# Two edits to the order of a mixture-of-experts and local-attention kernel: where the next token norms stand beside a softmax, and which queue loads the experts' second biases

## The chip, the cores and the metric

The kernel runs on one core of a Trainium2 chip. The core has a matrix engine (TensorE, "PE"), a vector engine (VectorE, "DVE"), a scalar engine (ScalarE, "ACT"), a general engine (GpSimd, "POOL") and a sync engine (SyncE, "SP"), each with an instruction queue of its own that it works through in order. SP, ACT and POOL can start DMA transfers; a transfer that has to wait for something holds everything behind it in the queue that issues it. The metric is the device time of one execution in microseconds (us).

## The reference

The input `x` is 16 x 256 tokens of 512 features, with a context tensor of the same shape and an index `itok` of a key position for each token. All is float32. Four residual layers follow each other, each behind a layer norm:

```
x = x + conv_attention(norm(x), k, skip, ctx)          # a long convolution over the features
x = x + experts(norm(x))                               # 8 experts, top 2, and a shared expert
x = x + local_attention(norm(x), ctx, itok)            # 16 heads, keys itok-8 .. itok
x = x + ffn(norm(x))                                   # 512 -> 2048 -> 512, gelu
```

The two layers that the change touches, cut to what matters:

```
# experts: the top 2 of 8 logits, softmax over the two
h = gelu(x @ w1[e] + b1[e])
routed = sum over the 2 experts of gate * (h @ w2[e] + b2[e])

# local attention
q_c = x @ W_dq;   kv_c = kv @ W_kvc
scores = (q_nope . k_nope + rope(q_rope) . rope(k_rope)) * scale
scores = where(itok - 8 <= key <= itok, scores, -1e30)
out = softmax(scores) @ v;   out @ W_o
```

## The kernel before, in words

The class `Kernel` writes one program. A scheduler puts the instructions of each engine in an order derived from the order in which they are written, and sets the waits between engines. The engine queues then run in that compiled order. `tc.issue_after(instruction)` around a piece of code makes what is written in it be placed behind the named instruction.

**Stages.** `conv_shared` does the first layer, the routing and the shared expert. `routed` runs the experts. `attention_sorted` does the local attention on tokens sorted by key position, and `ffn` the last layer. Data goes between the stages through DRAM: `x1d` holds the tokens after the first layer and the shared expert, `xgd` the normed rows grouped by expert, `ygd` the experts' results, `x3s` the tokens after attention.

**Around the bias load.** At its end `conv_shared` sends the last token rows to `xgd` by scattering (L437 on POOL's queue), writes zeros behind each expert's last row (eight scatters, also L437), and stores the tokens to `x1d` (L574, on SP's queue). `routed` then loads `e_b2`, the second biases of all experts for all 128 partitions, 2 MB, from a DRAM row that the kernel made before (L658 on VectorE is the last of the work that it waits for). Behind it come, on SP's queue, the expert tiles `xg`: `load` (L958) takes 128 rows of `xgd`, four tiles are in flight, and each load waits for the scatters of rows and zeros that could write them. PE transposes an expert tile (L972, `ptg`), multiplies it with `w1` (L983, `phg`), transposes the result (L994), ACT applies gelu (L996), and PE multiplies with `w2` (L1002, `pog`). The bias `b2` is added at the end (L1011) on VectorE, and the row stored to `ygd` (L1014). Between the expert tiles, `beside` prepares the attention's weights (loads `pre`, L1120).

**The attention.** There are 32 tiles T of 128 tokens, taken in groups of four. For one group: `tokens` makes the tile's input. It adds the two routed results, each times its gate, to the row of `x1d` (two L1542 on VectorE; the rows of `ygd` come by gathers on POOL's queue, L2005), takes the layer norm (L66, L68 and L72 on VectorE, L70 and L71 on POOL), transposes the rotary rows on PE (L1550, `prr`, copied at L1551) and the normed tile (L99, `pt`, copied by ACT at L100). `latents` makes the query latents (L1561, L1572), and `heads` makes the queries of two pairs of heads (L1589 to L1600 on PE; L1605 and L1613 copies on ACT; L1607 on VectorE; L1608 and L1609 on POOL).

For each tile, the loop in `attention_sorted` writes, in this order: `scores` (L1651, L1657 on PE), `weigh` (the first half of the softmax on VectorE: L1667 transpose, L1669 mask, L1673 maximum, L1674 subtraction), `tokens` of tiles of the next group, `values` of the tile before (L1697 `pu` on PE, copied at L1703), `weights` (the exponential, L1678 on ACT; the sum L1680, reciprocal L1682, product L1683 and transpose L1685 on VectorE), `window` of the tile after (key transposes, L1623 `pkw` and L1628 `prw` on PE; mask pieces L1636 to L1639 on VectorE), in the first two tiles the head pairs of the second half of group 0, and `project` of the tile two before (L1713 `po` on PE, 32 matmuls).

In the first group (g = 0) `tokens` of the next group's tiles is called for its tiles 0 and 1 at t = 1 and t = 2, and for its tiles 2 and 3 at t = 3. The scheduler is free to place the instructions of these calls on VectorE ahead of the softmax beside which they are written, as soon as their data is expected. In later groups the calls stand at another place (the end of the loop's body) and are not touched.

Of the kernel before, what the change touches and what calls it, by code (L numbers as in the profile page):

```python
# [13 lines left out]
ALU = mybir.AluOpType  # L14
# [4 lines left out]
P = 128  # L19
# [15 lines left out]
CQ, WIN = 8, 32  # L35
# [7 lines left out]
class Kernel:  # L43
# [888 lines left out]
    def routed(self, xgd, ygd, early):  # L932
        nc, tc, a = self.nc, self.tc, self.a
        with ExitStack() as ctx:
# [10 lines left out]
            ps_o = pool("e_ps_o", 2, space=PSUM)  # L945
            w1, w2 = self.e_w1, self.e_w2
            b2 = bp.tile([P, E, D], F32, name="e_b2")
            nc.sync.dma_start(b2, self.b2d.partition_broadcast(P))
            more = lambda i, half: self.beside(i, half, heads, early)

            def load(i):
# [24 lines left out]
            def hidden(i, xT):  # L976
                e = nc.values_load(
                    self.expert[0:1, i : i + 1], engines=[mybir.EngineType.PE], min_val=0, max_val=E - 1,
                    skip_runtime_bounds_check_because="a sum of a one-hot row over 0 to E - 1",
                )  # L980
                ph = ps_h.tile([P, EH], F32, tag="h", name="phg")
                for c in range(DC):
                    nc.tensor.matmul(  # L983
                        ph, xT[:, c, :], w1[:, c, bass.ds(e * EH, EH)], start=(c == 0), stop=(c == DC - 1)
                    )
                hs = tp.tile([P, EH], F32, tag="hs", name="hs")
                nc.vector.tensor_copy(hs, ph)
                return e, hs
# [30 lines left out]
            for i in range(NT):  # L1019
                if i + 2 < NT:  # L1020
                    xg[i + 2] = load(i + 2)
                e, hs = hidden(i, xT.pop(i))
# [452 lines left out]
    def attention_sorted(self, fetched, ygd, x3s, end_of_queries):  # L1475
        nc, tc = self.nc, self.tc
# [7 lines left out]
        with ExitStack() as ctx:  # L1484
# [50 lines left out]
            def tokens(st, t):  # L1535

                T = st["g"] * T4 + t
                if t == 0:
                    st["xT"], st["rope"] = g_xT, g_rope
                xt, yts, rr = xs[T], st["y"][t], rrs.pop(T)  # L1540
                for k in range(2):
                    nc.vector.scalar_tensor_tensor(  # L1542
                        xt, yts[k], self.routes[:, T, 2 + k : 3 + k], xt, ALU.mult, ALU.add
                    )
                xh = tp.tile([P, D], F32, tag="xh", name="xh")
                self.layernorm(xh, xt, small)
                toks = slice(t * P, (t + 1) * P)
                pt = ps_m.tile([P, 2, P], F32, tag="m", name="prr")
                for i in range(2):
                    nc.tensor.transpose(pt[:, i, :], rr[:, i, :], self.ident)  # L1550
                nc.scalar.copy(st["rope"][:, :, toks], pt)  # L1551
                self.transposed(st["xT"][:, :, toks], xh, ps_m, "m")
# [60 lines left out]
                        nc.scalar.copy(qn[:, cs, c0 : c0 + CQ], by_chunk(pqn[k][i]))  # L1613
                return turned

            wins, last_at = {}, [None]

            def window(T):
                gw = gws.pop(T)
# [21 lines left out]
            def scores(st, T):  # L1641

                w, t = wins[T], T % T4
                s = ps_s.tile([P, 4 * P], F32, tag="s", name="ps")
                for a in range(4):
                    for piece in range(3):
                        for j in range(4):
                            c = t * 16 + a * 4 + j
                            r = slice(j * WIN, (j + 1) * WIN)
                            if piece == 0:  # L1650
                                nc.tensor.matmul(  # L1651
                                    s[r, a * P : (a + 1) * P], w["kn"][:, a, r], qn[:, c, :],
                                    start=(a == 0), stop=False, skip_group_check=True,
                                )
                            else:
                                c0 = a * P + (piece - 1) * (P // 2)
                                nc.tensor.matmul(  # L1657
                                    s[r, c0 : c0 + P // 2], krz[piece - 1][:, a, r], qr[:, c, :],
                                    start=False, stop=True, skip_group_check=True,
                                )  # L1660
                return s

            def weigh(T, s):

                e = ap_.tile([P, 16, WIN], F32, tag="e", name="e")
                flat = e.rearrange("p x k -> p (x k)")
                nc.vector.transpose(flat, s)  # L1667
                e4 = e.rearrange("p (a h) k -> p a h k", h=4)
                nc.vector.tensor_tensor(  # L1669
                    e4, e4, wins[T]["mask"].unsqueeze(2).to_broadcast([P, 4, 4, WIN]), ALU.add  # L1670
                )
                mx = small.tile([P, 16], F32, tag="mx", name="mx")
                nc.vector.tensor_reduce(mx, e, AX.X, ALU.max)  # L1673
                nc.vector.tensor_tensor(e, e, mx.unsqueeze(2).to_broadcast([P, 16, WIN]), ALU.subtract)  # L1674
                return e

            def weights(e):
# [70 lines left out]
            for T in range(NT_ + 2):  # L1748
                g, t = T // T4, T % T4
                if T < NT_:  # L1750
                    if 3 <= T + 2 < NT_:
                        fetch_keys(T + 2)
                    s = scores(state[g], T)
                    e = weigh(T, s)
                    nxt = state.setdefault(g + 1, new(g + 1)) if g + 1 < NG else None

                    if nxt is not None:
                        for k in () if g == 0 else ((0,), (2,), (), ())[t]:
                            fetch((g + 1) * T4 + k)
                            fetch_routed(nxt, k)  # L1760
                    if nxt is not None and g == 0 and 1 <= t <= TH:
                        tokens(nxt, t - 1)
                    if nxt is not None and g == 0 and t == 3:
                        for k in range(TH, T4):
                            tokens(nxt, k)
                    if nxt is not None and t == 3:
                        latents(nxt)
                if 1 <= T <= NT_:
                    uts[T - 1] = values(T - 1, ats.pop(T - 1))
                if T < NT_:  # L1770
                    ats[T] = weights(e)
                    if T + 1 < NT_:
                        window(T + 1)
                    if T < 2:
                        for two in range(T * HP // 4, (T + 1) * HP // 4):
                            turned = heads(state[0], two, parts[1])
                    if nxt is not None and g == 0 and 1 <= t <= TH:
                        with tc.issue_after(turned):
                            fetch(T4 + TH + t - 1)
                            fetch_routed(nxt, TH + t - 1)  # L1780
                    if nxt is not None and t == 3:
                        for two in range(HP // 2):
                            heads(nxt, two)
                if T >= 2:
                    project(state[(T - 2) // T4], T - 2, uts.pop(T - 2))
                if T >= NT_:

                    if T == NT_:
                        end_of_queries()
                    which = T - NT_  # L1790
                    xT = self.e_w2[:, which * DC * N : (which + 1) * DC * N].rearrange("p (c x) -> p c x", c=DC)
                    for k in range(T4):
                        xt = ap_.tile([P, N], F32, tag="sw", name="xt", bufs=3)
                        nc.sync.dma_start(xt, x3s[which][k * P : (k + 1) * P, :])
                        xh = tp.tile([P, D], F32, tag="xh", name="xh")
                        self.layernorm(xh, xt, small)
                        self.transposed(xT[:, :, k * P : (k + 1) * P], xh, ps_m, "m")
                if T < NT_ and nxt is not None:
                    if g > 0:
                        if t == 0:  # L1800
                            fetch((g + 1) * T4 + 1)
                            fetch_routed(nxt, 1)
                        for k in ((0,), (1,), (2, 3), ())[t]:
                            tokens(nxt, k)
                        if t == 1:
                            fetch((g + 1) * T4 + 3)
                            fetch_routed(nxt, 3)
# [365 lines left out]
```

## Time and profile before

| | |
|---|---|
| median of 3 runs | 3021.12 us (3020.19 to 3021.73) |
| profiled execution | 3020.16 us, span 3018.4 us |
| PE busy | 2947.3 us (98%) |
| VectorE busy | 1461.7 us (48%) |
| POOL busy | 1112.7 us (37%) |
| ACT busy | 694.4 us (23%) |
| granted TensorE clock, mean | 0.995 |
| DMA | 209.87 MB, mean 70 GB/s |

The span is the time from the first to the last instruction of the profiled execution; its own time of 3020.16 us is 1.76 us longer. Rows of a list in order of time read: start, busy time, engine, line, operation, what it writes and reads, how many instructions were merged into the row, and in square brackets the idle time of the engine ahead of it with what ended it. All of these are in us from the start of the span. Rows of the granted clock give a share of full speed.

The bias load was issued at 902.58 and landed 9.1 us later. The attention's first tiles T = 0 to T = 3 stand at about 1278, 1298, 1315 and 1336 us.

### The profile page before, as it was taken

Reading aid. Unit: us, or ns where it says so; the run is one execution under the profiler, and the core shown is the slowest. Engines: PE = TensorE matmul, PEld = TensorE weight load, DVE = VectorE, ACT = ScalarE, POOL = GpSimd, SP = SyncE. Lnnn points to the kernel's source line nnn. Section 1 sums busy time; section 2 is a strip of 40 time slices with the busy share of each in tenths; the row PEclk is TensorE's granted clock in tenths of the full one; section 3 lists DMA queues with packets and bytes.
Section 4 is the critical chain, followed back from the end, with each engine's and each line's share of the span. In section 5 each row is a group of like instructions: output and inputs, shape, how many; then the busy total and the mean of one; then the engine's idle time right before and its main releaser. Section 6 shows DMA issues by size and latency. Waiting matters only on the chain.

```text
span 3018.4 us, 34924 instructions
## 1 busy us (share of the span) xinstructions
PE 2947.3 (98%) x12697; PEld 1499.5 (50%) x12697; DVE 1461.7 (48%) x2652; ACT 694.4 (23%) x1314; POOL 1112.7 (37%) x1462
## 2 busy tenths in 40 slices
PE   8999999999999999889999999999999999999998
PEld 4444444445446666544454455455444444444443
DVE  7978778778764444343343343343432223222222
ACT  2222112212211111333433333333211111111110
POOL 4566556455450300465555555543120300301101
PEclk9999999999999999999999999999999999999999
DMA  4231221221136733221131131112210100100100
GB/s 124 74 116 61 71 75 49 66 79 54 43 114 188 224 129 128 92 75 45 51 92 44 48 92 49 46 57 84 103 54 14 56 14 14 56 11 18 39 0 29
DMA packets 119219, 209.87 MB, mean 70 GB/s; under 512 B 27592, under 2 KB 47976, under 8 KB 118400
## 3 DMA queue, kind: packets, MB, share of 16 engines
q1 hardware_dynamic: 90752, 125.63, 13.9%
q0 software_dynamic: 28288, 81.92, 8.4%
q8 instruction: 104, 1.70, 0.2%
q14 instruction: 75, 0.61, 0.1%
HBM read 140.12 MB, written 67.37 MB: 69 GB/s over the span
## 4 chain that ended last, share of the span: by engine, by line
PE 80%; DVE 8%; issue 5%; POOL 4%; DMA 2%; ACT 0%; POOLq 0%; SPq 0%; DVEq 0%; ACTq 0%
PE po L1965 15%; PE ph L1907 13%; PE po L1713 11%; PE y L327 6%; PE phg L983 4%; PE pog L1002 4%; PE pqn L1592 4%; PE m L327 3%; PE pout L569 3%; PE ph L556 2%; PE pqr L1589 2%; DVE oT L332 2%; PE pqn L1600 2%; PE pt L99 2%; DVE kv L283 1%
## 5 line engine op out<-in xcount | busy, mean ns | idle before, releaser
L1713 PE MATMUL po<-nw,w 128*128 128x512 f32 x1024 | 445.7, 593 | 0.0
L1965 PE MATMUL po<-p,ht 128*128 128x512 f32 x1024 | 445.1, 592 | 0.0
L327 PE MATMUL y<-kv,ut 128*128 128x512 f32 x768 | 352.9, 595 | 9.3 <-DVE pr L338 9.3
L1713 PEld LDWEIGHTS po<-nw,w 128*128 128x128 f32 x1024 | 192.1, 190 | 235.1 <-issue 229.6
L1965 PEld LDWEIGHTS po<-p,ht 128*128 128x128 f32 x1024 | 192.7, 190 | 233.4 <-issue 232.0
L1907 PE MATMUL ph<-w,w 128*128 128x512 f32 x640 | 281.2, 592 | 0.0
L1969 DVE TENSOR_TENSOR res<-res,po 128x512 f32<-128x512 f32 x128 | 87.7, 685 | 315.4 <-PE po L1965 315.4
L327 PEld LDWEIGHTS y<-kv,ut 128*128 128x128 f32 x768 | 143.1, 191 | 183.3 <-issue 163.6
L1907 PEld LDWEIGHTS ph<-w,w 128*128 128x128 f32 x640 | 121.5, 190 | 152.6 <-issue 152.6
L283 DVE TENSOR_TENSOR kv<-pvt,cT 128x512 f32<-128x512 f32 x256 | 170.3, 682 | 0.5 <-PE pvt L267 0.5
L2005 POOL DMA_INDIRECT w<-ygd,slot_s x64 | 72.3, 1130 | 257.8 <-DMA pre<-in_W_uvT_dram 204.3
L2005 POOL DMA_INDIRECT gw<-kvd,keys_of x128 | 133.7, 1045 | 51.9 <-issue 37.3
L1607 DVE TENSOR_TENSOR w<-pqr,w 128x512 f32<-128x512 f32 (+1 forms) x72 | 45.3, 631 | 203.8 <-ACT sw L1605 188.1
L332 DVE TENSOR_REDUCE oT<-pr 128x64 f32<-128x512 f32 x192 | 131.8, 686 | 6.6
L983 PE MATMUL phg<-w,xTg 128*128 x568 | 134.6, 380 | 0.2
L1002 PE MATMUL pog<-w,hT 128*128 x284 | 133.6, 593 | 0.0
L70 POOL TENSOR_TENSOR ln_rs<-ln_mv,eps 128x1 f32<-128x1 f32 x64 | 13.0, 202 | 320.5 <-DVE ln_mv L68 316.0
L556 PE MATMUL ph<-xT,w_s 128*128 128x512 f32 x256 | 118.5, 607 | 0.0
L1921 ACT ACTIVATE ht<-ht,p1b 128x512 f32<-128x512 f32 x96 | 69.3, 722 | 212.8 <-DVE ht L1926 212.8
L293 POOL TENSOR_TENSOR w<-kv 128x512 f32<-128x512 f32 x64 | 81.2, 1269 | 100.0 <-DVE kv L283 70.8
L1592 PE MATMUL pqn<-w,m 128*128 128x512 f32 (+1 forms) x288 | 117.7, 552 | 0.3 <-DVE w L1569 0.3
L1907 PE MATMUL ph<-xT,w 128*128 128x512 f32 x256 | 116.4, 592 | 0.0
(305 smaller groups left out, 4509.1 us busy)
## 6 DMA issues: line engine op xcount, KB each, us to landing
xg<-xgd SPq DMA_DIRECT2D x71, 256.0 KB, 2.7
ygd<-y SPq DMA_DIRECT2D x71, 256.0 KB, 2.0
xt<-in_x_dram SPq DMA_DIRECT2D x32, 256.0 KB, 3.4
ct<-in_ctx_dram SPq DMA_DIRECT2D x32, 256.0 KB, 3.3
ut<-in_kt_dram SPq DMA_DIRECT2D x32, 256.0 KB, 2.7
w<-in_w_dram SPq DMA_DIRECT2D x8, 1024.0 KB, 5.8
x1d<-xt SPq DMA_DIRECT2D x32, 256.0 KB, 3.0
x3s<-xt POOLq DMA_DIRECT2D x32, 256.0 KB, 2.7
```

The source lines that it names most:

```text
L283: nc.vector.tensor_tensor(c["kv"][half][:, mc, :].rearrange("p (b j i) -> p b j i", i=NH, j=NH), c["vt"][:, mc, cols].rearrange("p (b i) - ...
L327: c["conv"] = nc.tensor.matmul(y, t, v, start=(start and k == 0), stop=(k == len(terms) - 1), skip_group_check=True).ins
L332: nc.vector.tensor_reduce(c["oT"][:, lc, cols].rearrange("p (b j) -> p b j", j=NH), pr, AX.X, ALU.add)
L556: nc.tensor.matmul(ph, w["sw1"][:, c, f * P : (f + 1) * P], xT[:, c, :], start=(c == 0), stop=(c == DC - 1),)
L569: nc.tensor.matmul(po, st["ht"][f][:, tok], w["sw2"][:, f, :], start=(f == 0), stop=(f == NC_ - 1))
L983: nc.tensor.matmul(ph, xT[:, c, :], w1[:, c, bass.ds(e * EH, EH)], start=(c == 0), stop=(c == DC - 1))
L1002: nc.tensor.matmul(po, hT[:, q, :], w2[:, bass.ds(e * (EH * D // P) + q * D, D)], start=(q == 0), stop=(q == EH // P - 1),)
L1592: nc.tensor.matmul(pqn[k][i], m0[:, 2 * hp + i, :], q0, start=True, stop=False)
L1713: nc.tensor.matmul(po, ut[:, n].rearrange("p a j q -> p (a j q)"), nw[:, 2 * hp + i, :], start=(n == 0), stop=(n == HEADS - 1),)
L1907: nc.tensor.matmul(ph, w[:, c, :], x[:, c, :], start=(start and c == 0), stop=(c == half - 1), skip_group_check=True,)
L1965: nc.tensor.matmul(po, ht[f, i // T4][:, toks], w2[:, f, :], start=(f == fs[0]), stop=(f == fs[-1]))
L2005: self.nc.gpsimd.indirect_dma_start(out=dst, out_offset=None, in_=src, in_offset=bass.IndirectOffsetOnAxis(ap=index, axis=0), bounds_check ...
```

## The change

Three places are edited. The load of `e_b2` in `routed` goes through ACT's DMA queue instead of SP's. `weigh` remembers its last subtraction (L1674). The loop of `attention_sorted` writes `tokens` of the next group's first two tiles, which it calls at t = 1 and t = 2 of the first group, inside `tc.issue_after` of that subtraction, so that their instructions stand behind the first half of the softmax of the same tile.

```diff
             b2 = bp.tile([P, E, D], F32, name="e_b2")
-            nc.sync.dma_start(b2, self.b2d.partition_broadcast(P))
+            nc.scalar.dma_start(b2, self.b2d.partition_broadcast(P))
...
-            wins, last_at = {}, [None]
+            wins, last_at, last_e = {}, [None], [None]
...
                 nc.vector.tensor_reduce(mx, e, AX.X, ALU.max)
-                nc.vector.tensor_tensor(e, e, mx.unsqueeze(2).to_broadcast([P, 16, WIN]), ALU.subtract)
+                last_e[0] = nc.vector.tensor_tensor(
+                    e, e, mx.unsqueeze(2).to_broadcast([P, 16, WIN]), ALU.subtract
+                ).ins
                 return e
...
                     if nxt is not None and g == 0 and 1 <= t <= TH:
-                        tokens(nxt, t - 1)
+                        with tc.issue_after(last_e[0]):
+                            tokens(nxt, t - 1)
```

## The prediction

> **What bounds the kernel now.** I read the page first: the busy times and the chain that ended last.
>
> ```profile
> span 3018.4 us, 34924 instructions
> PE 2947.3 (98%) x12697; PEld 1499.5 (50%) x12697; DVE 1461.7 (48%) x2652; ACT 694.4 (23%) x1314; POOL 1112.7 (37%) x1462
> PE 80%; DVE 8%; issue 5%; POOL 4%; DMA 2%; ACT 0%; POOLq 0%; SPq 0%; DVEq 0%; ACTq 0%
> ```
>
> TensorE is busy 2947.3 of 3018.4 us, so 71.1 us of idle is all that a change of order can win. A move matters only where it takes out or opens a hole on PE. I then listed PE in order of time around the edited places. For the attention edit (T = 0, 1, 2, 3 are its first four tiles):
>
> ```profile
> 1292.40 1.22 PE L1589 MATMUL pqr<-w,w_qr 128*128 128x256 f32 x2 [5.96 <-DVE w L1607]
> ...
> 1297.84 0.42 PE L1651 MATMUL ps<-w,kn 128*32 128x128 f32 x8
> ...
> 1300.01 0.60 PE L99 MATMUL pt<-ident,xh 128*128 128x128 f32 x4
> ...
> 1319.09 0.64 PE L99 MATMUL pt<-ident,xh 128*128 128x128 f32 x2
> 1319.66 1.17 PE L1697 MATMUL pu<-at,gw 32*128 32x128 f32 x32
> ...
> 1340.45 0.63 PE L99 MATMUL pt<-ident,xh 128*128 128x128 f32 x4 [1.93 <-DVE xh L72]
> ...
> 1351.34 0.66 PE L1628 MATMUL prw<-ident,gw 128*128 128x128 f32 x4 [2.33 <-DVE w L1569]
> ```
>
> One hole of 5.96 us stands ahead of the second head pair of T = 0. The two transposes of normed tokens (L99, at 1300.01 and 1319.09) cost no wait: their norms were done early. After 1351.34 PE has no hole over 0.4 us until 1790, so time lost here is not made good later. VectorE in the same stretch shows why the hole exists:
>
> ```profile
> 1279.52 0.75 DVE L1542 SCALAR_TENSOR_TENSOR xt<-w,routes,xt 128x512 f32<-128x512 f32 x1 [6.99 <-DMA w<-ygd,slot_s]
> ...
> 1285.77 0.71 DVE L1667 STREAM_TRANSPOSE e<-ps 128x512 f32<-128x512 f32 x1
> ...
> 1299.88 0.72 DVE L1667 STREAM_TRANSPOSE e<-ps 128x512 f32<-128x512 f32 x1 [1.52 <-PE ps L1657]
> ...
> 1320.81 0.75 DVE L1542 SCALAR_TENSOR_TENSOR xt<-w,routes,xt 128x512 f32<-128x512 f32 x1 [6.74 <-DMA w<-ygd,slot_s]
> 1321.48 0.71 DVE L1667 STREAM_TRANSPOSE e<-ps 128x512 f32<-128x512 f32 x1
> ```
>
> The scores of T = 0 are done at 1279.5, but four token sums (L1542), paced by gathers, stand ahead of the softmax, which starts at 1285.77. For the clock, the stretches 1286.5 to 1292.4 (the hole) and 1292.4 to 1300 (columns: length, PE, PE loads, DVE, ACT, POOL, PEclk, DMA, GB/s):
>
> ```profile
> 1286.50:1292.40 5.90, 0.00 (x0) 0.00 (x0) 5.19 (x14) 2.77 (x8) 2.28 (x4) 0.70 0.00 0
> 1292.40:1300.00 7.60, 7.60 (x118) 6.07 (x119) 3.09 (x7) 3.19 (x10) 4.99 (x7) 0.79 0.01 2
> ```
>
> For the bias edit, SP's waits from 850 to 935 and PE and SP in order of time:
>
> ```profile
> SPq L948 <- DVE bias L658: 22.5, 1, 22.5
> SPq L958 <- DMA xgd<-zero,t_ends: 3.5, 1, 3.5
> ```
> ```profile
> 902.58 0.33 SPq L948 DMA_DIRECT2D e_b<-b2d  x1
> 905.22 3.95 SPq L574 DMA_DIRECT2D x1d<-xt  x2
> 914.15 1.28 SPq L958 DMA_DIRECT2D xg<-xgd  x2
> ```
> ```profile
> 916.91 0.66 PE L972 MATMUL ptg<-ident,xg 128*128 128x128 f32 x4 [2.14 <-DMA xg<-xgd]
> 918.63 0.63 PE L972 MATMUL ptg<-ident,xg 128*128 128x128 f32 x4 [1.06 <-DMA xg<-xgd]
> ```
>
> PE stands 3.20 us for the first two expert tiles. They wait for the last scatter of zeros into the same DRAM rows (landed 913.89), not for SP to be free.
>
> **The change, part by part.** *The second biases (L948).* The 2 MB load waits on either queue for the same L658 and starts at 902.6. On ACT's queue it stands behind the last shared gelu (ends 901.9) and ahead of L996 (922.34); ACT idles 20.5 us there, so its wait holds nobody. On SP it had held everything behind it for 22.5 us. The compiled order now puts the first four xg loads ahead of four x1d stores that stood before and between them. The load's 9.1 us and the zeros' landing stay; what goes is two stores (landed 913.37 and 914.73) competing with the zeros, and a store between xg loads 2 and 3. I estimate the zeros 0.65 us earlier and the second xg load landing at 917.2 for 918.49: **−1.3 us**. Bounds: the whole hole, −3.2, and a slight loss, +0.5, if b2 and zeros collide otherwise. The Trainium skill ("DMA: Bandwidth & Descriptors", Issuing engines are not separate DMA queues) says that SP, ACT and POOL share 16 engines and a change of issuer saves only issue time. The rows fit: one zero scatter landed at 911.87, beside b2's 911.64, against 2.9 to 3.6 us for scatters before it. By the rule alone the queue change gives 0; I keep 1.3 because the order of stores and loads changes too. Xg loads 5 to 7 come some 3 us later, and the stores later still; tile 5 lands by 927.5 and is needed at about 931.
>
> *T = 0.* The token sums leave; the softmax starts at 1279.6, exp at 1283.2 (after its table load, 1281.90 + 1.28), L1607 at 1285.3 for 1291.93. The pair takes 4.65 us, like its neighbours, for 12.72 (1285.12 to 1297.84): −8.07, and 0.30 before 1282.13: **−8.3 us**. The clock's share is in it.
>
> *T = 1.* The compiled order of VectorE puts token 0 behind L1674. PE's order is as before: prr, pt of that token, and only then pu, pkw, prw and the next head pair. PE is in order, so all of these wait. Scores end at about 1291.5. The chain: softmax to L1674 2.95 (as 1299.88 to 1302.83), a mask piece 0.25, two L1542 1.35, L1680 0.66, L66 0.66, a reciprocal and L68 0.42, POOL's L70 and L71 with their hand-overs 1.08, L72 0.55: 7.9 us minus 0.4 by overlaps of starts. So pt starts at about 1299.0 against 1300.01: **−1.0** in total there, the gain of T = 0 being eaten by a new hole of about 7.2 us. Behind it, slow clock +1.6 (below), and the 0.85 us before 1304.03 (ACT w L1703, held by an exp that now comes earlier) goes. Running sum: −1.0 + 1.6 − 0.85 = **−0.2**.
>
> *T = 2.* Token 1 now stands behind this softmax. That softmax is itself late: two gathers for token 2 land at 1320.8 and 1322.3, and their sums stand ahead of L1667 and L1669. By the rows of before (shifted by −0.2): L1674 ends 1325.2, two L1542 1326.8, L1680 1327.4, L66 1328.0, L68 1328.2; POOL's L70 is behind two gathers that wait for the same sums and end at 1328.8; L71 ends 1329.7, L72 1330.3. So pt comes at 1330.4 for 1319.09, and behind it wait pu, pkw, prw and the 13.9 us of L1713: a new hole of **+11.3 us**. PE's scores there need nothing from it.
>
> *The clock.* After the hole of 5.96 us the granted clock was 0.79 over 7.6 us and the pair took 5.44 for 4.65: 0.8 us lost. The Trainium skill ("TensorE: Matmul & The Clock Gate", Part 1) says that an idle window of about 3.4 us halves the clock until a busy window has passed. By the row two holes cost 1.6; by the rule each full window at half speed costs 1.7, two windows 3.4. The work behind the new holes (L1713's full-width matmuls above all) is denser than that pair, so I take 1.6 and **+2.1**; bounds 0.8 and 3.4 each.
>
> *T = 3.* Holes there are of VectorE work that the PE delay of 13 us overtakes: the 1.93 before 1340.45 shrinks by 1.7, and 2.33 before 1351.34 with 0.17 beside it goes: **−4.2**. If POOL's gathers move back with PE, this is 0.
>
> **Sum** against the profiled execution, span 3018.4, time 3020.16 (1.76 outside the span): −1.3 − 0.2 + 11.3 + 2.1 − 4.2 = +7.7, span 3026.1, time 3027.9. The median of the runs, 3021.12, lies 0.96 above that execution: **3028.8 us**.
>
> **Rivals.**
> - *Token 1's hole is short (ends on the other side: no change).* If gathers for token 2 land before the scores end, the softmax of T = 2 starts at 1319.1 for 1321.48 and loses L1542's two places: the hole is 8.0, the clock 1.5: 3021.12 − 1.3 − 0.2 + 8.0 + 1.5 − 4.2 = 3024.9. It decides below a hole of 9.7 us. For it: POOL issues are rough in the trace. Against: the gathers stand at the same place in POOL's order.
> - *PE's clock and POOL are worse.* Both holes cost 3.4 (+3.1), or T = 3 gives nothing back (+4.2): 3031.9 to 3033.0. For it: windows of half clock of 6.8 us stand at 1288.83.
> - *The biases gain nothing.* The scatter of zeros still lands at 913.9: 3030.1.
> - *Faster.* PE doesn't wait for pt because another release is inferred wrongly and token 1's norm is done by 1319: −8.3 and −1.3 with neither hole: about 3012. Against: the queue order is compiled, and PE doesn't pass over L99.
>
> **How the numbers follow.** Forecast with the case of no gain from the biases 0.53, short hole 0.22, worse clock or POOL 0.21, faster 0.04. A measurement of this kernel tells about 0.2% (6.0 us) from no change. Slower than 3027.16: nearly all of the first (0.49) and all of the third: 0.70; within: 0.26; faster: 0.04. The range goes from inside the short hole, 3023.0, to 3033.0.
>
> **What would show it.** In the changed kernel: no hole at L1589 of T = 0 and VectorE's L1667 at 1279.6; a hole of 7 us before the first L99 behind T = 1's scores and of 11 us before that of T = 2, both released by DVE xh L72, a lower granted clock after each; the holes of 1.93 and 2.33 gone; the first xg hole under 2.1 and 1.06. It is wrong if L99 of T = 2 waits less than 9.7 us, or if PE passes it.

## The result, and the profile after

The changed kernel takes 3030.57 us (median of 10 runs, 3026.80 to 3032.17); before takes 3021.30 us beside it (10 runs). The ratio is 1.0028, 95% interval 1.0020 to 1.0037: slower by some 9 us, where 3028.8 us (+7.7) was forecast, inside the range of 3023 to 3033. The profiled execution took 3030.07 us, its span is 3028.3 us, 9.9 us more than before.

The page of the changed kernel, first the busy times, then the chain that ended last:

```profile
span 3028.3 us, 34922 instructions
...
PE 2947.0 (97%) x12697; PEld 1500.7 (50%) x12697; DVE 1461.8 (48%) x2652; ACT 695.0 (23%) x1314; POOL 1114.5 (37%) x1462
...
PE 80%; DVE 8%; issue 5%; POOL 4%; DMA 2%; ACT 1%; POOLq 0%; SPq 0%; DVEq 0%; ACTq 0%
```

PE is busy as long as before (2947.0 for 2947.3 us), so all of the 9.9 us is idle time in the sum. PE in order of time, in the attention's first four tiles, shows where it lies. Two lines are new: L1697 of before is L1699 here, L1713 is L1715.

```profile
1284.46 1.27 PE L1589 MATMUL pqr<-w,w_qr 128*128 128x256 f32 x4
...
1289.16 0.43 PE L1651 MATMUL ps<-w,kn 128*32 128x128 f32 x8
...
1299.49 1.09 PE L99 MATMUL pt<-ident,xh 128*128 128x128 f32 x4 [7.99 <-DVE xh L72]
1300.51 2.09 PE L1699 MATMUL pu<-at,gw 32*128 32x128 f32 x32
...
1313.23 0.44 PE L1550 MATMUL prr<-ident,rr 128*128 128x128 f32 x2
...
1331.48 1.09 PE L99 MATMUL pt<-ident,xh 128*128 128x128 f32 x4 [13.28 <-DVE xh L72]
1332.50 2.09 PE L1699 MATMUL pu<-at,gw 32*128 32x128 f32 x32
...
1335.72 13.90 PE L1715 MATMUL po<-nw,w 128*128 128x512 f32 x32
...
1360.89 0.66 PE L1628 MATMUL prw<-ident,gw 128*128 128x128 f32 x4
1361.38 1.88 PE L1589 MATMUL pqr<-w,w_qr 128*128 128x512 f32 x4
```

The hole of 5.96 us at T = 0 is gone: L1589 of the second pair comes as one row of four, and the scores of T = 1 start at 1289.16 for 1297.84. In its place stand holes of 7.99 and 13.28 us, both ahead of the token transposes (L99), both ended by L72. The holes of 1.93 and 2.33 us at T = 3 are gone too (no bracket at 1360.89).

VectorE and POOL at T = 2, each in order of time:

```profile
1321.28 0.75 DVE L1542 SCALAR_TENSOR_TENSOR xt<-w,routes,xt 128x512 f32<-128x512 f32 x1 [6.76 <-DMA w<-ygd,slot_s]
1321.94 0.71 DVE L1667 STREAM_TRANSPOSE e<-ps 128x512 f32<-128x512 f32 x1
...
1325.05 0.68 DVE L1674 TENSOR_TENSOR e<-e,mx 128x512 f32<-128x512 f32 x1
1325.66 0.74 DVE L1542 SCALAR_TENSOR_TENSOR xt<-w,routes,xt 128x512 f32<-128x512 f32 x1
...
1330.79 0.55 DVE L72 TENSOR_SCALAR xh<-xt,ln_mv,ln_rs 128x512 f32<-128x512 f32 x1 [1.53 <-POOL ln_rs L71]
```
```profile
1328.88 1.00 POOL L2008 DMA_INDIRECT w<-ygd,slot_s  x1 [0.31 <-DVE ln_mv L68]
1329.91 0.20 POOL L70 TENSOR_TENSOR ln_rs<-ln_mv,eps 128x1 f32<-128x1 f32 x1
```

The links are those of the forecast: the softmax waits for a sum whose gather lands late, token 1's sums come behind L1674, and POOL's L70 stands behind a gather. The granted clock around the new holes (columns as before, the clock is the third figure from the end):

```profile
1290.00:1300.00 10.00, 2.01 (x73) 1.71 (x62) 8.42 (x18) 2.20 (x6) 3.44 (x6) 0.71 0.01 2
1300.00:1305.00 5.00, 5.00 (x47) 4.37 (x45) 0.14 (x1) 2.97 (x6) 1.70 (x2) 0.56 0.06 13
...
1330.00:1336.00 6.00, 4.52 (x45) 3.91 (x46) 4.72 (x11) 1.98 (x4) 3.97 (x6) 0.57 0.32 85
```

Behind each hole PE works at little more than half clock: pu takes 2.09 us for 1.17. PE's busy time doesn't grow by it, since slow stretches of before are gone: the pair behind the old hole, and the scores of T = 2, whose last rows took 0.67 us each in before and take 0.41 here. At the expert tiles, PE and SP:

```profile
915.02 0.66 PE L972 MATMUL ptg<-ident,xg 128*128 128x128 f32 x4 [1.25 <-DMA xg<-xgd]
916.35 0.63 PE L972 MATMUL ptg<-ident,xg 128*128 128x128 f32 x4 [0.67 <-DMA xg<-xgd]
918.10 3.23 PE L983 MATMUL phg<-w,xTg 128*128 x8 [1.13 <-DVE xTg L973]
```
```profile
912.35 3.05 SPq L958 DMA_DIRECT2D xg<-xgd  x4
```

The four loads are issued in one run, and the holes in front of the first two tiles are 1.92 us for 3.20. But a third hole of 1.13 us follows, and the first product (L983) takes 3.23 us for 1.99, at a clock of 0.59 while it runs.

### The profile page after: what moved, and what is told of

It is laid out like the page before. It is cut to its first block, busy times and chain, and to the rows that moved or that the text cites. A ratio compares the mean times of both kernels' runs of the same rounds, so it can differ in the third digit from the quotient of the medians.

```text
span 3028.3 us, 34922 instructions
## 1 busy us (share of the span) xinstructions
PE 2947.0 (97%) x12697; PEld 1500.7 (50%) x12697; DVE 1461.8 (48%) x2652; ACT 695.0 (23%) x1314; POOL 1114.5 (37%) x1462
## 4 chain that ended last, share of the span: by engine, by line
PE 80%; DVE 8%; issue 5%; POOL 4%; DMA 2%; ACT 1%; POOLq 0%; SPq 0%; DVEq 0%; ACTq 0%
PE po L1968 15%; PE ph L1910 13%; PE po L1715 9%; PE y L327 6%; PE phg L983 4%; PE pog L1002 4%; PE pqn L1592 4%; PE m L327 3%; PE pout L569 3%; PE ph L556 2%; PE pqr L1589 2%; DVE oT L332 2%; PE pqn L1600 2%; PE pt L99 2%; DVE kv L283 1%
## 5 line engine op out<-in xcount | busy, mean ns | idle before, releaser
L1715 PE MATMUL po<-nw,w 128*128 128x512 f32 x1024 | 445.7, 593 | 0.0
L1715 PEld LDWEIGHTS po<-nw,w 128*128 128x128 f32 x1024 | 192.0, 190 | 235.1 <-issue 229.6
L1607 DVE TENSOR_TENSOR w<-pqr,w 128x512 f32<-128x512 f32 (+1 forms) x72 | 45.5, 632 | 209.8 <-ACT sw L1605 188.8
L983 PE MATMUL phg<-w,xTg 128*128 x568 | 135.8, 382 | 1.1 <-DVE xTg L973 1.1
L70 POOL TENSOR_TENSOR ln_rs<-ln_mv,eps 128x1 f32<-128x1 f32 x64 | 13.8, 216 | 322.7 <-DVE ln_mv L68 316.4
```

The lines of the kernel that those rows point to most:

```text
L983: nc.tensor.matmul(ph, xT[:, c, :], w1[:, c, bass.ds(e * EH, EH)], start=(c == 0), stop=(c == DC - 1))
L1715: nc.tensor.matmul(po, ut[:, n].rearrange("p a j q -> p (a j q)"), nw[:, 2 * hp + i, :], start=(n == 0), stop=(n == HEADS - 1),)
```

## The experiments

The runs form four studies, each group of them on one chip and compared with before on that chip. In the first three before took 3053 to 3056 us; in the last, as at the prediction, 3021. The traces of those three studies show what the 32 us are made of, at least in part: PE waits for its own issue (time in which it waited for nothing that the profile shows), or for VectorE, which itself stands still there (10.6 us ahead of L987) with no engine of this core named as the cause. These are PE's waits from 960 to 1380 us in the kernel with the biases alone (line, releaser, us in total, times, longest):

```profile
PE phg L983 <- DVE xTg L973: 8.0, 1, 8.0
PE pth L994 <- DVE hs L987: 6.0, 1, 6.0
PE ps L1657 <- issue: 4.2, 10, 1.0
```

None of these three stands among before's waits in that stretch at the prediction. The sizes of the holes differ there too: PE came to T = 0 some 22 us later, and in the three traces with the attention as before the hole of T = 0 was 2.60, 0.54 and 2.48 us and not 5.96, which takes most of the change's gain away. In the first of them:

```profile
1311.01 0.70 PE L1589 MATMUL pqr<-w,w_qr 128*128 128x256 f32 x2 [2.60 <-DVE w L1607]
...
1314.86 0.43 PE L1651 MATMUL ps<-w,kn 128*32 128x128 f32 x8
```

So those studies tell which hole belongs to which part; the totals at before's 3021 us come from the result and the last study. The attention edit alone was not measured at 3021.

**Both parts apart.** The attention edit alone keeps the biases on SP's queue; the biases alone leave the attention as before.

```diff
 # behind_alone, behind_alone_2: the change without
-            nc.scalar.dma_start(b2, self.b2d.partition_broadcast(P))
+            nc.sync.dma_start(b2, self.b2d.partition_broadcast(P))
 # b2_alone, b2_alone_2: before with
-            nc.sync.dma_start(b2, self.b2d.partition_broadcast(P))
+            nc.scalar.dma_start(b2, self.b2d.partition_broadcast(P))
```

> Only the tokens' work goes behind the softmax; the biases stay on SP's queue. The forecast's steps for the attention sum to +9.0 us: 3030.3 us. If the changed kernel's whole +9.3 us comes from here and the biases gain nothing, 3030.6 us; if the biases gained 1.3 us in it, 3031.9 us. In either case a hole of about 8 us ahead of the token transposes (L99) of T = 1 and of about 13 us ahead of those of T = 2.

> The attention edit alone once more, beside before on the same chip. In the first study both kernels ran on a chip where TensorE waited some 17 us more for its own next instructions in the experts' stage and before more than once in the attention, so that the sizes of the holes were not those of the prediction. Without such waits: +9.0 us by the forecast's steps, +9.3 to +9.6 if the biases gave the change nothing; the holes 8 us and 13 us, both released by L72. With them: +16 us as in the first study.

Measured: 3069.00 us for 3053.08 (ratio 1.0054, 1.0040 to 1.0067) and 3071.69 for 3055.84 (1.0052, 1.0038 to 1.0066): +15.9 and +15.9. PE in the first:

```profile
1326.27 1.09 PE L99 MATMUL pt<-ident,xh 128*128 128x128 f32 x4 [8.00 <-DVE xh L72]
...
1362.33 1.09 PE L99 MATMUL pt<-ident,xh 128*128 128x128 f32 x4 [11.41 <-DVE xh L72]
```

The two holes come from this part alone; the size of the first is that of the changed kernel to 0.01 us. The expected +9 was missed, since the gain at T = 0 is mostly absent there.

> Only the load of the second biases goes to ACT's queue; the attention stays as before. The forecast's step says -1.3 us, 3020.0 us, with the first two expert tiles' holes on PE together under 2.0 us instead of 3.2. The rival reading, from the trace of the changed kernel, where the tiles landed earlier but PE then ran at a lower granted clock: 0 +- 0.5 us, 3021.3 us, and the first matmuls of expert tile 0 (L983) take more than 2.0 us. If the load collides with the scatters of zeros, it is slower, up to 3022.

> The biases alone once more. The forecast's step: -1.3 us. The rival: 0 +- 0.5 us, because PE's clock takes back what the earlier landing gives.

Measured: 3051.05 for 3053.08 (0.9996, 0.9988 to 1.0005) and 3054.62 for 3055.84 (0.9998, 0.9989 to 1.0006): -2.0 and -1.2 us by the medians (the ratios give -1.2 and -0.6), neither clear of zero. The stage itself can be read in every trace, as the time from the start of the last shared outputs (L569) to the second L983. Eight traces with the load on SP's queue have 21.5 to 23.1 us, mean 22.3; five with it on ACT's 20.0 to 23.8, mean 21.7. The spread is the clock's: in the three traces on ACT's queue where L983 ran in 1.99 us, the stage took 20.0, 20.9 and 21.1 us, in the other two 22.5 and 23.8; on SP's queue it took 21.5 twice at full clock, and 22.0 to 23.1 in the six others. At like clock the edit is worth about 0.8 us at full clock and nothing at the reduced one (two traces against six). The two holes ahead of the first tiles (L972) came to 2.4 to 3.2 us, mean 2.9, with the load on SP's queue, and to 1.7 to 2.4, mean 2.0, with it on ACT's: the tiles did land sooner, by about 0.9 us.

**The load of the biases behind the first tiles.**

```diff
 # b2_late: before with
-            nc.sync.dma_start(b2, self.b2d.partition_broadcast(P))
...
             xg = {0: load(0), 1: load(1)}
+            nc.sync.dma_start(b2, self.b2d.partition_broadcast(P))
```

> The attention as before; the load of the second biases stays on SP's queue but is written behind the loads of the first two expert tiles. If the load's 2 MB is what delays the scatters of zeros and so the first expert tiles, these land up to 3 us earlier and the hole of 3.2 us mostly goes: 3018.3 to 3019.3 us. If the hole is set by something else (the scatters' own descriptors, or PE's clock behind it), within 1 us of 3021.3 us. If the biases are then late for their first add (L1011), slower than 3022 us.

Measured: 3055.95 for 3053.08 (1.0006, 0.9997 to 1.0014), no gain. PE at the first three tiles (its lines are one less than before's):

```profile
914.39 1.04 PE L971 MATMUL ptg<-ident,xg 128*128 128x128 f32 x8
915.93 1.99 PE L982 MATMUL phg<-w,xTg 128*128 x8 [0.51 <-DVE xTg L972]
921.56 0.63 PE L971 MATMUL ptg<-ident,xg 128*128 128x128 f32 x4 [3.63 <-DMA xg<-xgd]
```

The first two tiles have no hole at all: the 2 MB load did delay them. But the third tile now waits 3.63 us: putting the load behind two tiles moves the wait to the third. In this run the DMA engines are 1.00 busy from 910 to 925 us, so the transfer finds no idle stretch there.

**The token transposes behind the other work of the tile.**

```diff
 # late_turns, late_turns_keys: the attention edit alone, with
-                            tokens(nxt, t - 1)
+                            turn_late = tokens(nxt, t - 1, late=True)
...
                     project(state[(T - 2) // T4], T - 2, uts.pop(T - 2))
...
+                if T < NT_ and nxt is not None and g == 0 and 1 <= t <= TH:
+                    turn_late()        # L1550, L99 and their copies
```

> As the attention edit alone, but the two PE transposes of each moved token tile (L1550, L99 in before) are written at the end of the loop's body, behind the head pairs of T = 1 and the projection of T = 2. The theory says that the loss comes from PE's own order, which stands in front of a late norm: both new holes then vanish while the hole of T = 0 stays gone: -8.3 us and -0.85 us, less up to 4 us given back at T = 3: 3012 to 3016 us. The rival says that the norms themselves are late for the next group, and the wait only moves to T = 3 (latents): over 3022 us, with a hole of over 8 us ahead of L1561 or of a L99 of T = 3.

> The token transposes at the end of the loop's body once more. In the first study this version removed the two waits for L72 but opened one of 3.68 us at T = 1: VectorE's L1607 stood behind L72, and L72 behind POOL's L70 and L71, which stood behind four key gathers (gw). Without waits for instructions: 3021.3 - 8.3 - 0.85 + 3.7 + 1.0 (clock) = 3017 us if PE's order was the cause of the loss; over 3024 if the wait only moves to T = 3.

Both are the same kernel. Measured: 3053.98 for 3053.08 (1.0002, 0.9994 to 1.0010) and 3056.33 for 3055.84 (1.0003, 0.9995 to 1.0011): 15 us better than the attention edit alone in the same studies, equal to before, and short of the gain expected. Only the place where the two transposes and their copies are written differs from the attention edit alone, so PE's order is shown as the cause of its loss. The missing gain is mostly that of T = 0: with the 2.60 us of this chip in place of the 8.3, the second expectation's sum gives about +1 us (an estimate: -2.6 - 0.85 + 3.7 + 1.0), where +0.9 was measured beside it. No L99 of T = 1 or T = 2 waits any more. A new hole stood at T = 1; PE, VectorE and POOL around it in the first of the two:

```profile
1326.16 1.22 PE L1594 MATMUL pqr<-w,w_qr 128*128 128x256 f32 x2 [3.68 <-DVE w L1612]
```
```profile
1323.21 0.94 DVE L72 TENSOR_SCALAR xh<-xt,ln_mv,ln_rs 128x512 f32<-128x512 f32 x1 [1.64 <-POOL ln_rs L71]
...
1325.72 0.72 DVE L1612 TENSOR_TENSOR w<-pqr,w 128x256 f32<-128x256 f32 x2
```
```profile
1321.30 1.00 POOL L2015 DMA_INDIRECT gw<-kvd,keys_of  x1 [0.30 <-issue]
1322.33 0.20 POOL L70 TENSOR_TENSOR ln_rs<-ln_mv,eps 128x1 f32<-128x1 f32 x1
```

L1612 (L1607 of before) stands behind L72, L72 behind L71, and L70 behind four key gathers. So these were put behind the norm:

```diff
 # keys_behind_norm: late_turns, and at T = 1 and T = 2
-                        fetch_keys(T + 2)       # ahead of the scores
...
                             turn_late = tokens(nxt, t - 1, late=True)
+                        with tc.issue_after(self.normed):
+                            fetch_keys(T + 2)
```

> Token transposes at the end of the loop's body, and at T = 1 and T = 2 the key gathers (gw) behind the token's L71 on POOL's queue instead of ahead of it. The theory says that the version without this gave back its gain in a hole of 3.68 us at T = 1, because L72 and with it L1607 waited for L71 behind four gathers, and in the half clock behind that: now 4 to 5 us less than that version: before -4 us. The rival, that the gain is lost at T = 3 whatever comes before: before +-1 us, with the holes at T = 3 (L99, L1628) longer by what T = 1 saves.

Measured: 3051.65 for 3053.52 (0.9993, 0.9985 to 1.0001): -1.9 us, between the two expectations, its interval just including no change. The hole at L1594 is 2.10 us, so it shrank by 1.6 and not by 3.7: what is left is VectorE's own work ahead of L1612, the sums, the norm and the second half of the softmax.

**Only token 0 behind the softmax.**

```diff
-                        with tc.issue_after(last_e[0]):
-                            tokens(nxt, t - 1)
+                        if t == 1:
+                            with tc.issue_after(last_e[0]):
+                                tokens(nxt, t - 1)
+                        else:
+                            tokens(nxt, t - 1)
```

> Only token tile 0 goes behind the softmax (of T = 1); token tile 1 is left to the scheduler, which puts its two sums ahead of the softmax of T = 0. If the two holes add, this shows the share of T = 1: a hole of 8 us ahead of the first L99 and none over 1 us ahead of the second, and about half of the loss of the attention edit alone: +7 us on chips like those of the first two studies (+3 on one like the prediction's). If the loss is all of T = 2's: within 2 us of before.

Measured: 3058.68 for 3053.52 (1.0016, 1.0009 to 1.0023): +5.2 us, against +15.9 for both tokens. PE at the two L99:

```profile
1325.38 1.09 PE L99 MATMUL pt<-ident,xh 128*128 128x128 f32 x4 [7.50 <-DVE xh L72]
...
1349.07 0.69 PE L99 MATMUL pt<-ident,xh 128*128 128x128 f32 x2
```

A hole for token 0, none for token 1. So token 0's move, the small gain at T = 0 included, makes about a third of the loss. The other two thirds come with token 1's; no run moved token 1 alone.

**PE kept busy in the holes.**

```diff
 # fill: the attention edit alone, with, ahead of the token transposes
+        for k in range(fill):                    # 16 at T = 1, 24 at T = 2
+            nc.tensor.matmul(
+                pt.rearrange("p c x -> p (c x)"), self.ident, self.nw[:, k % HEADS, :], start=True, stop=True
+            )
```

> The attention edit alone, with matmuls of no use (identity times rows of the output weights, 16 at T = 1 and 24 at T = 2, 0.43 us each as L1713's) into the PSUM tile that the token transposes then overwrite, so that PE computes while it waits for L72. The waits stay as long. The theory says that the two holes cost their length and, behind them, 3.4 us of half clock (1.8 behind T = 1, 1.6 behind T = 2 in the changed kernel): with PE kept busy it is 3 us faster than the attention edit alone, that is before +12.5 us on chips like those of the first two studies, before +6 us on one like the prediction's. The rival, no clock effect: the same as the attention edit alone or slower by what the useless matmuls overrun (+16 or +9.3).

Measured: 3079.93 for 3053.52 (1.0085): +26.4 us. The total says nothing on the clock, because the useless matmuls were mis-sized: each is two of PE's records, 0.87 us and not 0.43, and they overran the holes.

```profile
1318.96 13.90 PE L99 MATMUL pt<-nw,ident 128*128 128x512 f32 x32
1332.69 0.60 PE L103 MATMUL pt<-ident,xh 128*128 128x128 f32 x4
1333.22 1.17 PE L1703 MATMUL pu<-at,gw 32*128 32x128 f32 x32
...
1379.63 0.60 PE L103 MATMUL pt<-ident,xh 128*128 128x128 f32 x4
1380.16 1.17 PE L1703 MATMUL pu<-at,gw 32*128 32x128 f32 x32
...
1382.19 13.90 PE L1719 MATMUL po<-nw,w 128*128 128x512 f32 x32
```

But the work behind them can be timed. From the transposes to the second head pair of T = 1 it is 6.75 us here (1332.69 to 1339.44), and 9.04 in the changed kernel (1299.49 to 1308.53): 2.3 us less. From the transposes of T = 2 to po it is 2.56 us here and 4.24 there: 1.7 less. The attention edit alone, on a chip of these studies, has 9.06 and 3.98, which gives 2.3 and 1.4. The same instructions, kept behind a busy PE, run at full clock (1.00 in both stretches).

**The changed kernel again, and a version that beats both.** The last is keys_behind_norm with the biases on ACT's queue.

> The changed kernel itself, on a chip of the studies, where before takes some 3054 us and not 3021. The attention edit alone cost +16.0, +15.9 us there, the biases alone -2.0 and -1.2. If the two parts add: before +14 us (+13 to +15). If the biases' part gives nothing in company: +16.

> The version with the late token transposes and the key gathers behind the norms (before -1.9 us in its study), with the biases on ACT's queue as well (-2.0 and -1.2 alone). If the parts add: before -3.5 us, faster than both kernels. If the biases do nothing: before -2 us.

Measured, with before at 3020.82 us: the changed kernel 3029.53 (1.0030, 1.0018 to 1.0042), +8.7 us. The other 3012.89 (0.9973, 0.9963 to 0.9983), **-7.9 us**: clear of before, and 16.6 us below the change. Both expectations were written for the conditions of the other studies; under those of the prediction the gain at T = 0 is there to be kept. How the 16.6 us divide between the transposes and the gathers was measured only in the other studies (15, then some 2.5 us). PE in the version that wins:

```profile
1301.72 0.70 PE L1594 MATMUL pqr<-w,w_qr 128*128 128x256 f32 x2 [2.09 <-DVE w L1612]
...
1315.61 13.90 PE L1720 MATMUL po<-nw,w 128*128 128x512 f32 x32
1329.35 0.38 PE L1555 MATMUL prr<-ident,rr 128*128 128x128 f32 x2
1329.57 0.60 PE L99 MATMUL pt<-ident,xh 128*128 128x128 f32 x4
```

po of T = 2 starts at 1315.61, 6.1 us ahead of before's 1321.70 and 20.1 ahead of the change's, though its attention had started 1.1 us later than before's (pkw at 1280.53 for 1279.44). Token 1's transposes come behind po and wait for nothing. Holes of 0.55, 1.50 and 1.12 us remain at T = 3.

## Why the prediction was right

Against before, PE stood as follows in the changed kernel (each figure is the growth of the difference between the two kernels' starts since the point above it). In the second row stands the gain of T = 0, forecast -8.3, measured -8.6 at the scores of T = 1.

| point | forecast | measured |
|---|---|---|
| the biases, at pkw of T = 0 | -1.3 | -0.1 |
| T = 0 and T = 1, to the second L1550 | -0.2 | +0.5 |
| T = 2, to its L99 | +11.3 | +12.0 |
| clock behind it, to po | +2.1 | +1.6 |
| T = 3, to L1589 | -4.2 | -4.5 |
| sum | +7.7 | +9.5 |

The span grew by 9.9 us; the last 0.4 came later. Point by point:

- *T = 0.* Right: the pair took its neighbours' time once the softmax stood in front, and the scores of T = 1 began at 1289.16.
- *T = 1.* The norm's chain ended at 1299.35, where 1299.0 was forecast; the hole was 7.99 for 7.2. The clock cost 2.3 us behind it by the comparison with fill (1.8 by before's own rows, with its 0.85 us wait taken out), where 1.6 was taken.
- *T = 2.* Right in each link, and 0.7 us short. Of this 0.2 is a slip in the sum: 1330.4 already held the shift of -0.2 that the sum takes off again. The rest is POOL's: the last gather ahead of L70 ended at 1329.88, where 1328.8 was forecast. The hole itself was 13.28 and not 11.3, because these scores ran at full clock and ended at 1318.20 for 1319.16, while the chain ended no sooner. A hole counted between two moving ends is not the loss; the start of L99 is. late_turns, which moved only PE's transposes and their copies, shows that it is PE's order that makes VectorE's delay cost.
- *The clock.* The row of before was misread. Its 5.44 us behind the hole were set against the 4.65 of a whole pair, but part of the pair had run ahead of the hole. The same matmuls behind the hole of 2.60 us, at clock 1.00, took 3.85 us (1311.01 to 1314.86, shown above). So the row gives 1.6 us for a hole and not 0.8, some 3.2 for two. That agrees with the estimate of 3.4 from the rule of the Trainium skill ("TensorE: Matmul & The Clock Gate", Part 1), and the measured 2.3 + 1.7 us lie a little above both. The 3.7 that was taken, above the rule and far above the row as it was read, was nearly it, partly by luck: the reason given for it, denser work, wasn't tried.
- *T = 3.* Right: PE arrived later and the waits were over.
- *The biases.* This is the term that was mis-sized. The mechanism held: two tiles landed sooner, and their holes shrank by 1.3 us. But PE did not get on sooner. From L569 to the second L983 it took 22.48 us for before's 21.51, because another hole and a clock of 0.59 behind it took more back; that PE had come to L569 1.0 us earlier, at work ahead of the edited place, hides this in the -0.1. Before's profile is one of the two of eight at full clock here, the changed kernel's one of the two of five that are not, so this pair of traces alone is no fair measure of the edit. The clock behind these holes was left out of the term, though it was counted in the others. The runs put the edit between 0 and -2 us; more is not settled. The case "the biases gain nothing", 3030.1 us, came nearest of all to the measured 3030.57.

The misses of the rows are +1.2, +0.7, +0.7, -0.5 and -0.3 us, so part of them cancels in the sum.

The rival of a short hole at T = 2 did not come up, since the first gather for token 2 landed where it did before (its sum starts at 1321.28 for 1320.81).

## What to carry to other kernels

An instruction moved behind others on one engine also moves what waits for it on an engine that runs in order: before a norm is put later, see where the reader of its result stands in PE's queue, and move that too. The two edits together gained 8 us once the two transposes went behind the tile's other work and the key gathers behind the norm; without that they cost 9. Where a wait on PE is shortened, count the clock behind it as well: holes that closed by 1.3 us were followed by a clock of 0.59 here. To price a slow clock, set the same instructions side by side, not a part against a whole.

## What the runs showed of the hardware that had not been expected

- The same kernel took 3021 us in some studies and 3053 to 3056 in others, on different chips, each steady within 8 us. In the slower ones PE, VectorE and SP stood still or issued in fits while POOL's gathers followed each other: with the biases alone, VectorE did nothing from 1008.8 to 1019.4 us and SP issued nothing from 1009.1 to 1021.6, beside gathers every 1.3 us. In the attention edit alone, PE's scores of T = 2 ran so while POOL issued gathers from 1343.34 to 1352.3 us:

```profile
1345.35 0.33 PE L1657 MATMUL ps<-w,krz 128*32 128x64 f32 x5 [0.41 <-issue]
1346.08 0.32 PE L1657 MATMUL ps<-w,krz 128*32 128x64 f32 x4 [0.40 <-issue]
```

  At the prediction the same scores beside the same gathers ran without a stop. That the gathers are the cause is not shown, and what differs between the chips wasn't tried.
- The granted clock behind a hole of about 2 us in the experts' stage was full in some executions (0.36 us to L983 and 1.99 for it, clock 1.00) and reduced in others (3.23 us, clock 0.59), with the same kernel. With that, the stage took 21.11 and 22.48 us.
